# Halves of an exchange, and transposes by blocks, in a two-layer attention kernel on one Trainium2 core

## Chip, core and metric

The kernel runs on one core of one Trainium2 chip. All arithmetic is in 32-bit floats. The metric is device time in microseconds (us): 1245.21 in the median of three runs, 1244.89 to 1247.77.

## What is computed

Two layers act on x, 8 batches of 128 rows of 512. Layer 0 picks an adapter weight for each batch and adds a small mixture of low-rank experts. Layer 1 is attention with a paged cache of keys and values, and behind it a gated network; this is where the change lies:

```python
q = rmsnorm(x @ Wq.T, q_norm_w)          # 32 heads of 128
k = rmsnorm(x @ Wk.T, k_norm_w)          # 8 heads of 128
v = x @ Wv.T
q, k = rope(q, pos), rope(k, pos)
k_all = concat([k_cache[block_table], k])    # 512 cached + 128 new
v_all = concat([v_cache[block_table], v])
probs = softmax(where(valid, q @ k_all.T * SCALE, -1e30))
y = (probs @ v_all) @ Wo.T

scores = (y @ Wq_w.T) @ keys.T           # 64 experts, top 16
gate = softmax over the 16 best, 0 elsewhere
z_gated = (y @ A_w.T) * gate             # 8 columns for each expert
out = x + z_gated @ B_w.T * SCALING
```

## The kernel before

**Units.** Layer 0 takes the first 114 us or so. Then a loop runs over 64 units: a unit is one batch and one group of heads (four query heads with their key head). Two units make a step `st` (two groups, GH = 2); a step is one batch, and the 8 batches are gone through four times, once for each pair of groups. `iteration(u)` works on several units at once: scores and softmax of unit u (`scores`, `mask_exp`, `normalize`), norms and rotation of unit u + 3, the values of unit u - 2 (`values`, TensorE), and the output product of unit u - 3 (`evict_o` and `output`). In between, the projections of later units run on TensorE (`project`, seven products of halves instead of eight; L259, L262, L265). Iterations alternate: the even one has three of these products, the odd one four. An even one takes 15.9 us, an odd one 17.2 us.

**The exchange.** Probabilities have queries on partitions and TensorE wants them with keys on partitions. VectorE turns them in blocks of 32x32 (`blocks`, L833, 128x640 each, four heads) into the tile `pb`; the blocks of q and k for unit u + 2 go to the end of the same tile (`blocks_qk`, L784). `exchange_out` (L847) writes the tile to DRAM (`px`) with four transfers of 400 KB, two on SP's queue and two on ScalarE's, at the end of iteration u. `exchange_in` of the next iteration reads back `qkb` (L857, 320 KB) and `pT` (L860, 1280 KB) on SP. `heads_qk` (L867) copies qkb on ScalarE into the form that the scores take. `evict_o` (L891) is ScalarE's copy of the values' result out of PSUM, which the output product y (L902) needs; ScalarE comes to it behind its two px writes of the iteration before.

**SP's queue.** In every iteration SP issues, in this order: three transfers of the next step's keys (`gather`, L194, 32 KB each; 16 in a step, ten in an even and six in an odd iteration), qkb, pT, the rest of the gathers, a load of the running output in even ones (`load_y`, L143), its store (`add_output`, L926), and its two px writes. The values' rows come by GpSimd's indirect transfers (L204), and so do the weights of the next heads (wqkv, wo) in some iterations.

**The end.** For the last pair of groups a step's y is complete, and the gated network begins while the loop still runs: `f_turn` turns y by four TensorE transposes (L684) and a ScalarE copy (L686), `f_project` makes the expert scores and z (L692, L701), `f_gate` (L712 to L733, VectorE, with one exponential on ScalarE, L724) picks the experts and multiplies, `z_turn` turns z (L746, L748), and `f_second` makes the result (L1147). `LAST` says in which iteration each batch's part comes (u = 59 to 65); the last batch comes behind the loop. `TURNED`, `gate` and the functions `turn_*` are new.

Of the kernel before, what the change touches and what calls it, by code (L numbers as in the profile page):

```python
# [31 lines left out]
NQ = HKV // GH  # L32
HW = NH // 2 * D + D
QD = P // 32
PW = REP * (LC + 1) * 32
XW = PW + NH * 32
EPS = 1e-6
SCALE = D ** -0.5
E1, R1, RD = 64, 8, 16
# [18 lines left out]
def adaln_ffn_kernel(  # L58
# [124 lines left out]
    def gather(step, first=0, end=NPP):  # L183
        hf, b = divmod(step, B)
        if first == 0:
            kv_t[step] = (
                kvp.tile([P, NPP, GH, PSIZE], F32, tag="kt", name=f"kt_{step}"),
                kvp.tile([P, LC, GH * D], F32, tag="vt", name=f"vt_{step}", bufs=3),
            )
        kt, vt = kv_t[step]  # L190
        for j in range(first, end):
            at = b * NPP + j
            page = nc.sync.value_load(pg[0:1, at : at + 1])
            nc.sync.dma_start(  # L194
                out=kt[:, j, :, :].rearrange("p g t -> p (g t)"),
                in_=kc[hf, ds(page, 1)].rearrange("o p f -> p (o f)"),
            )
# [473 lines left out]
    def f_fold(psum):  # L671
# [5 lines left out]
            )  # L677
        nc.vector.tensor_copy(fw_t["s"], rk)

    def f_turn(b, sb, psum):  # L680
        yb = ya_t.pop((NQ - 1) * B + b)
        tp = psum("tp", [P, NC, S])
        for c in range(NC):
            nc.tensor.transpose(tp[:, c, :], yb[:, c * P : (c + 1) * P], ident)  # L684
        yT = sb("yT", [P, NC, S])
        nc.scalar.copy(yT, tp)  # L686
        return yT
# [52 lines left out]

    zT_t = {}

    def z_turn(b, tp, sb):
        zg = zg_t.pop(b)
        for c in range(NC):
            nc.tensor.transpose(tp[:, c * S : (c + 1) * S], zg[:, c * P : (c + 1) * P], ident)  # L746
        zT = sb("zT", [P, NC, S])
        nc.scalar.copy(zT.rearrange("p c s -> p (c s)"), tp)  # L748
        zT_t[b] = zT


    with ExitStack() as l1:
# [6 lines left out]
        )  # L759

        p_t, pb_t, pT_t, den_t, o_t, oT_t, y_t = {}, {}, {}, {}, {}, {}, {}
        mask_t, px_t, qkb_t, qk_out = {}, {}, {}, {}

        def make_mask(st):
            b = st % B
# [2 lines left out]
            mask_t[st] = m  # L768

        def new_pb(u):  # L770

            if u < 2:
                pb_t[u] = wk1.tile([P, QD, PW], F32, tag=f"pT{u}", name=f"pb_{u}")
                return
            pb_t[u] = wk1.tile([P, QD, XW], F32, tag="pb", name=f"pb_{u}")

        def blocks_qk(u, w):

            if w == 1:
                gap = xo[:, 0, 4:].rearrange("p x c s -> p (x c s)")[:, : NH * S]  # L780
                qk_out[w] = gap.rearrange("p (i f) -> p i f", i=QD)
            else:
                qk_out[w] = pb_t[w][:, :, PW:]
            nc.vector.transpose(  # L784
                qk_out[w].rearrange("p i (h a) -> p h i a", a=32),
                qk_t.pop(u).rearrange("p h t d -> p h (t d)").rearrange(
                    "p h (i a) -> p h i a", a=32
                ),
            )
# [40 lines left out]
        def blocks(u, h):  # L830

            w = (LC + 1) * 32
            nc.vector.transpose(  # L833
                pb_t[u][:, :, h * w : (h + 1) * w].rearrange("p i (j a) -> p j i a", a=32),
                p_t.pop((u, h)).rearrange("p (j i a) -> p j i a", i=QD, a=32),
            )

        def exchange_out(u):

            pb = pb_t.pop(u)  # L840
            m = dram_x.tile([QD, 32, QD, XW], F32, tag="px", name=f"px_{u}")
            w = XW if u + 2 in range(3, NU) else PW
            for i in range(QD):
                eng = nc.sync if i < QD // 2 else nc.scalar
                for n, end in ((PW, w), (0, PW)) if u == 1 else ((0, w),):
                    src = qk_out[u] if n else pb[:, :, :end]
                    (nc.sync if n else eng).dma_start(  # L847
                        out=m[:, :, i, n:end].rearrange("k b f -> b k f"),
                        in_=src[i * 32 : (i + 1) * 32],
                    )  # L850
            px_t[u] = m

        def exchange_in(u):
            m = px_t.pop(u).rearrange("k b i f -> (k b) i f")
            if u + 2 in range(3, NU):
                qkb = wk1.tile([P, QD, NH * 32], F32, tag="qkb", name=f"qkb_{u + 2}")
                nc.sync.dma_start(out=qkb, in_=m[:, :, PW:])  # L857
                qkb_t[u + 2] = qkb
            pT = wk1.tile([P, QD, PW], F32, tag=f"pT{u % 2}", name=f"pT_{u}")
            nc.sync.dma_start(out=pT, in_=m[:, :, :PW])  # L860
            pT_t[u] = pT

        def heads_qk(u):
# [46 lines left out]
        def add_output(u):  # L910
            st, g = units[u]
            del oT_t[u]
            if g % GH < GH - 1:
                return
            y = y_t.pop(st)
            last = st >= (NQ - 1) * B
            if g < GH:
                ya_t[st] = yp.tile([P, DM], F32, tag="ya", name=f"ya_{st}")
                nc.vector.tensor_copy(ya_t[st], y)
            else:  # L920

                t = y_home[st % B] if last and st % B < 4 else ya_t[st]
                nc.vector.tensor_tensor(t, y, ya_t[st], ALU.add)
                ya_t[st] = t
            if not last:
                nc.sync.dma_start(out=y_d[st % B], in_=ya_t.pop(st))  # L926

# [1 line left out]

        LAST = {NU - 5 + b: b for b in range(B - 1)}  # L930
        y_home, yT_t, room_t = {}, {}, {}

        def rooms():
            w = wp.tile([P, 7 * 2 * HW], F32, tag="wqkv", name="rooms", bufs=GH)
# [38 lines left out]
            (2, 3): (1, 1, 1),  # L973
        }

        def iteration(u):

            on = lambda v: 0 <= v < NU
# [17 lines left out]
            first, end = ((0, 10), (10, NPP))[u % GH]  # L996
            if pages:
                gather(st + 1, first, first + 3)
            if on(u - 1):
                exchange_in(u - 1)  # L1000
            if pages:
                gather(st + 1, first + 3, end)
            if pages:
                gather_v(st + 1, u % GH * LC // GH, (u % GH + 1) * LC // GH)
            if on(u + 3) and u % GH == 1:
                make_tables(units[u + 3][0])
            if u % GH == 0 and B <= st - 1 < NQ * B:
                load_y(st - 1)
            if on(u - 3):
                evict_o(u - 3)  # L1010
            if u >= NU and fb is not None:
                yT_t[fb] = f_turn(fb, *f)
            if u > NU:
                z = u - NU - 1
                z_turn(z, bank("q" if z else "kv", f"ztp_{z}"), lambda n, shape: y_home[
                    z
                ].rearrange("p (c s) -> p c s", c=NC))
            for h in range(REP):
                if on(u):
                    scores(u, h)  # L1020
                    mask_exp(u, h)
                    if h > 0:
                        normalize(u, h - 1)

                    if h == 1:
                        if u == 2:
                            rotate(4)
                        elif u == 3:
                            sums_q(1, 3, 2)
                        elif u == 4:  # L1030
                            sums_q(1, 4, 1)
                        elif r in (10, 11, 12, 13) and u < NU - 8:
                            sums_q(group + r // 12, *((3, 2), (4, 1))[r % 2])
                    if h == 2:
                        new_pb(u)
                        if u + 2 in range(3, NU):
                            blocks_qk(u + 2, u)
                    if h > 1:
                        blocks(u, h - 2)
                    if h == 1 and u == NU - 5:  # L1040
                        f_fold(f[1])
                    if h == 2 and fb is not None:
                        yT_t[fb] = f_turn(fb, *f)
                if on(u - 3):
                    output(u - 3, h)
                if h > 0 and slots:
                    project(k, j, slots[h - 1 : h])

                if (u, h) in WHOLE:
                    project_whole(1, *WHOLE[u, h])  # L1050
            if on(u - 3):
                add_output(u - 3)
            if on(u + 1) and (u + 1) % GH == 0:
# [21 lines left out]
            if on(u):  # L1075
                blocks(u, REP - 2)
                blocks(u, REP - 1)
                exchange_out(u)
            if 4 < u + 3 < NU:
                rotate(u + 3)  # L1080
                if four and slots:
# [6 lines left out]
                y_home.update({b: t[:, b * DM : (b + 1) * DM] for b in range(4)})  # L1088
            if u == NU - 6:
                rooms()  # L1090
            if fb is not None:
                f_gate(fb, *f_project(fb, yT_t.pop(fb), *f), *f)
            if on(u - 2):
                values(u - 2)

        make_mask(0)
# [5 lines left out]
    with ExitStack() as l2:  # L1102
# [31 lines left out]
        def f_turn_z(t):  # L1134
            b = t
            sb = lambda n, shape: p2.tile(shape, F32, tag=n, name=f"f{n}_{b}")
            z_turn(b, bank("q" if t % 2 else "kv", f"ztp_{t}"), sb)

        def f_second(t):
            b = t  # L1140
# [114 lines left out]
```

## Time and profile before

| | |
|---|---|
| median of three runs | 1245.21 us (1244.89 to 1247.77) |
| profiled execution | 1245.7 us |
| its span | 1243.9 us (1.8 us lie around it) |
| TensorE (PE) busy | 1225.7 us, 99% of the span, 3847 matmuls |
| VectorE (DVE) busy | 901.9 us, 73% |
| ScalarE (ACT) busy | 506.5 us, 41% |
| GpSimd (POOL) busy | 590.9 us, 48% |
| granted TensorE clock | 0.998 |
| moved by DMA | 298.99 MB in 205505 packets, 240 GB/s in the mean |

PE, DVE, ACT, POOL and SP are TensorE, VectorE, ScalarE, GpSimd and SyncE. A line such as `L847 ACTq DMA_DIRECT2D px<-pb` is the issue of a transfer on that engine's queue, from tile pb to tile px, by line 847. In the lists of groups the numbers behind x are counts, and behind the bar stand busy time, mean ns of one, and the idle time of the engine just before, with what ended most of it. In the list of waits the numbers are total us, times, longest us. In the list of issues the last number is the median from issue to landing.

### The profile page before, as it was taken

To read this page: it belongs to the slowest core of one execution; us is meant where nothing else is said; L and a number is where in the kernel's file an instruction comes from. 1 tells how busy PE (TensorE), PEld (TensorE's weight loads), DVE (VectorE), ACT (ScalarE), POOL (GpSimd) and SP (SyncE) were. 2 spreads that over 40 slices of the span, in tenths; PEclk is the share of its full clock that TensorE was granted. 3 is DMA by queue.
4 is the path that set the end of the run, shared out by engine and by line. 5 is a ranking of instruction groups with operands and counts; after the bars stand their busy time and mean duration, and the time that the engine had idled before them with its cause. 6 is when DMAs were issued, how large, how long until landed. Compare 5 with 4: busy or idle time off the path is not lost.

```text
span 1243.9 us, 15998 instructions
## 1 busy us (share of the span) xinstructions
PE 1225.7 (99%) x3847; PEld 651.1 (52%) x3847; DVE 901.9 (73%) x2045; ACT 506.5 (41%) x1457; POOL 590.9 (48%) x687
## 2 busy tenths in 40 slices
PE   8999899999999999999999999999999999999998
PEld 7765455554555555545555545554555555555444
DVE  3546788888877777788877777788777777777522
ACT  1334444444444444444444444444444444443211
POOL 2443565576544444565545545555555444543100
PEclk9999999999999999999999999999999999999999
DMA  8822777788877887788878878888888877787512
GB/s 302 304 78 94 229 234 245 245 274 281 269 243 245 272 258 239 259 295 278 269 248 267 264 221 258 294 272 267 257 268 262 255 243 233 246 261 269 179 51 85
DMA packets 205505, 298.99 MB, mean 240 GB/s; under 512 B 84643, under 2 KB 117156, under 8 KB 204516
## 3 DMA queue, kind: packets, MB, share of 16 engines
q1 hardware_dynamic: 173812, 205.58, 52.6%
q10 hardware_dynamic: 18720, 52.32, 12.0%
q0 software_dynamic: 12880, 40.08, 9.7%
q8 instruction: 31, 0.51, 0.2%
q14 instruction: 62, 0.51, 0.1%
HBM read 183.54 MB, written 114.36 MB: 239 GB/s over the span
## 4 chain that ended last, share of the span: by engine, by line
PE 89%; DMA 4%; DVE 2%; ACT 1%; issue 1%; POOL 1%; SPq 1%; ACTq 0%; DVEq 0%; POOLq 0%
PE o L880 19%; PE p L259 19%; PE y L902 17%; PE s L798 16%; PE s L801 4%; PE bp L517 2%; PE op L1147 2%; PE p L292 2%; PE cp L495 2%; PE fz L701 2%; DMA kt<-in_kc 1%; DMA bww<-in_base_w 1%; DMA px<-pb 1%; PE cp L512 1%; DMA pT<-px 1%
## 5 line engine op out<-in xcount | busy, mean ns | idle before, releaser
L828 POOL TENSOR_SCALAR p<-p,den 128x640 f32<-128x640 f32 x256 | 211.8, 827 | 424.4 <-DVE den L827 423.8
L822 ACT ACTIVATE p<-p,low 128x640 f32<-128x640 f32 x256 | 211.9, 828 | 436.3 <-DVE den L827 295.6
L811 DVE CUSTOM_DVE_ANT_0 p<-s,mask,rs 128x640 f32<-128x640 f32 x256 | 223.5, 879 | 108.8 <-PE s L801 106.1
L259 PE MATMUL p<-wqkv,xo 128*128 128x384 f32 x784 | 280.5, 487 | 0.0
L902 PE MATMUL y<-wo,oT 128*128 128x512 f32 x512 | 262.8, 598 | 7.6 <-ACT oT L891 7.4
L798 PE MATMUL s<-kt,qkT 128*128 128x512 f32 x504 | 258.9, 595 | 1.5 <-DVE low L811 0.8
L880 PE MATMUL o<-pT,vt 128*128 128x512 f32 x512 | 230.2, 593 | 0.0
L833 DVE STREAM_TRANSPOSE pb<-p 128x640 f32<-128x640 f32 x256 | 211.0, 824 | 16.9 <-POOL p L828 16.9
L259 PEld LDWEIGHTS p<-wqkv,xo 128*128 128x128 f32 x784 | 149.1, 190 | 139.8 <-issue 72.3
L801 PEld LDWEIGHTS s<-qkT 128*128 128x128 f32 x504 | 96.2, 191 | 121.0 <-issue 121.0
L880 PEld LDWEIGHTS o<-pT,vt 128*128 128x128 f32 x512 | 97.5, 190 | 110.1 <-issue 95.0
L204 POOL DMA_INDIRECT vt<-in_vc,vrow x128 | 136.3, 1065 | 37.4 <-issue 28.2
L798 PEld LDWEIGHTS s<-kt,qkT 128*128 128x128 f32 x504 | 95.4, 191 | 96.7 <-issue 54.0
L308 ACT ACTIVATE sq<-c 128x128 f32<-128x128 f32 x320 | 98.8, 309 | 8.1
L314 POOL TENSOR_TENSOR rs<-ss,mhalf 128x5 f32<-128x5 f32 x64 | 99.5, 1554 | 5.3
L801 PE MATMUL s<-qkT 128*128 128x128 f32 x504 | 97.2, 275 | 0.0
L891 ACT COPY oT<-o 128x512 f32<-128x512 f32 x64 | 37.4, 585 | 144.9 <-PE o L880 133.6
L902 PEld LDWEIGHTS y<-wo,oT 128*128 128x128 f32 x512 | 78.6, 192 | 14.2 <-ACT oT L891 9.7
L262 DVE TENSOR_TENSOR c<-c,p 128x384 f32<-128x384 f32 x84 | 45.3, 539 | 28.8 <-PE p L259 28.7
L880 PE MATMUL o<-pT,vn 128*128 128x512 f32 x128 | 65.4, 592 | 0.0
L308 ACT ACTIVATION_READ_ACCUMULATOR sq<-c 128x1 f32 x320 | 59.7, 187 | 0.0
L340 DVE SCALAR_TENSOR_TENSOR ca<-c,rs,tab 128x128 f32<-128x128 f32 x64 | 24.8, 387 | 45.1 <-POOL rs L314 45.1
(181 smaller groups left out, 1200.7 us busy)
## 6 DMA issues: line engine op xcount, KB each, us to landing
pT<-px SPq DMA_DIRECT2D x64, 1280.0 KB, 6.7
px<-pb ACTq DMA_DIRECT2D x120, 400.0 KB, 5.3
px<-pb SPq DMA_DIRECT2D x120, 400.0 KB, 5.5
qkb<-px SPq DMA_DIRECT2D x61, 320.0 KB, 3.5
kt<-in_kc SPq DMA_DIRECT2D x512, 32.0 KB, 4.4
wqkv<-in_wqkv POOLq DMA_DIRECT2D x32, 384.0 KB, 5.4
yd<-ya SPq DMA_DIRECT2D x24, 256.0 KB, 3.1
wo<-in_wo POOLq DMA_DIRECT2D x12, 512.0 KB, 4.7
```

Source lines behind the costliest of these rows:

```text
L204: nc.gpsimd.indirect_dma_start(out=kv_t[step][1][:, c, :], out_offset=None, in_=vc, in_offset=bass.IndirectOffsetOnAxis(ap=vrow[:, hf, at ...
L259: nc.tensor.matmul(out=ps, lhsT=xo[:, pr, x, c, :], rhs=w[:, c, :], start=(c == 0), stop=(c == 1))
L308: nc.scalar.activation(sq, cs[:, at : at + D], AF.Square, accum_out=ss[:, h : h + 1])
L314: nc.gpsimd.tensor_tensor(rs, ss, mhalf, ALU.pow)
L798: nc.tensor.matmul(out=s[:, :L], lhsT=qkT[:, h, :], rhs=kt[:, :, g % GH, :], start=True, stop=True)
L801: nc.tensor.matmul(out=s[:, L:NK], lhsT=qkT[:, h, :], rhs=qkT[:, REP, :], start=True, stop=True)
L811: nc.vector.tensor_tensor_reduce(out=p, in0=s_t.pop((u, h))[:, :NK], in1=mask_t[st], scale=rs_t[u][:, h : h + 1], scalar=BIG, op0=ALU.add, ...
L822: nc.scalar.activation(p, p, AF.Exp, bias=low, scale=-1.0, accum_out=den)
L828: nc.gpsimd.tensor_scalar(p_t[u, h], p_t[u, h], den, 1.0, ALU.mult, ALU.mult)
L833: nc.vector.transpose(pb_t[u][:, :, h * w : (h + 1) * w].rearrange("p i (j a) -> p j i a", a=32), p_t.pop((u, h)).rearrange("p (j i a) -> ...
L880: nc.tensor.matmul(out=o, lhsT=vt[:, c, j * D : (j + 1) * D] if c < LC else vn_t.pop(u), rhs=pT[:, c], start=(c == 0), stop=(c == LC),)
L902: nc.tensor.matmul(out=y_t[st], lhsT=oT_t[u][:, h, :], rhs=wo_t[g][:, h, :], start=(h == 0 and j == 0), stop=(h == REP - 1 and j == GH - 1),)
```

## The change

Four things change.

1. The tile pb becomes two: pb_a (the blocks of q and k, and heads 0 and 1) and pb_b (heads 2 and 3). The first half is written out in the iteration's fourth head, two transfers on SP and two on ScalarE; the second half at the end of the iteration on SP, and in the next iteration on ScalarE, behind `evict_o`. So eight writes take the place of four. In the next iteration SP reads qkb behind three gathers, and pT behind all of them.
2. Six of the eight y and six of the eight z are turned without TensorE: VectorE turns blocks, four SP transfers write them to DRAM in the next iteration, one reads them back, and a ScalarE copy puts them in order.
3. The gate of a batch comes an iteration later, behind head 1's mask exponential; from u = 64 on at the start, with the values of the last units ahead of the projections.
4. y is always added into its own tile; the first two units' blocks have no tiles of their own any more.

```diff
+TURNED = B - 2
+def turn_blocks(n, rows, room, pool):
+    nc.vector.transpose(
+        room.rearrange("p (k c a) -> p c k a", k=QD, c=NC),
+        rows.rearrange("p (c k a) -> p c k a", c=NC, k=QD),
+    )
+    blocks_t[n] = pool, room
+def turn_out(n):
+    pool, room = blocks_t.pop(n)
+    m = pool.tile([QD, 32, QD, NC * 32], F32, tag="yx", name=f"yx_{n}")
+    for i in range(QD):
+        nc.sync.dma_start(out=m[:, :, i].rearrange("k b f -> b k f"),
+            in_=room[i * 32 : (i + 1) * 32].rearrange("p (k f) -> p k f", k=QD))
+    return n, m, room
+def turn_in(n, m, room):
+    nc.sync.dma_start(
+        out=room.rearrange("p (i f) -> p i f", i=QD), in_=m.rearrange("k b i f -> (k b) i f"))
+    turned_t[n] = room
+def turn_chunks(n, out):
+    nc.scalar.copy(out.rearrange("p c (i a) -> p c i a", a=32),
+        turned_t.pop(n).rearrange("p (i c a) -> p c i a", i=QD, c=NC))
 def f_turn(b, sb, psum):
+    if ("y", b) in turned_t:
+        yT = sb("yT", [P, NC, S])
+        turn_chunks(("y", b), yT)
+        return yT
...
         def new_pb(u):
-            if u < 2:
-                pb_t[u] = wk1.tile([P, QD, PW], F32, tag=f"pT{u}", name=f"pb_{u}")
-                return
-            pb_t[u] = wk1.tile([P, QD, XW], F32, tag="pb", name=f"pb_{u}")
+            pb_t[u] = (
+                wk1.tile([P, QD, XA], F32, tag="pb_a", name=f"pba_{u}"),
+                wk1.tile([P, QD, XW - XA], F32, tag="pb_b", name=f"pbb_{u}"),
+            )
...
-        def exchange_out(u):
+        def exchange_out(u, half, engines=(nc.sync, nc.scalar)):
...
-            pT = wk1.tile([P, QD, PW], F32, tag=f"pT{u % 2}", name=f"pT_{u}")
+            pT = wk2.tile([P, QD, PW], F32, tag="pT", name=f"pT_{u}")
...
+        def gate(fb):
+            b = fb - 1
+            part, f = gate_t.pop(b)
+            f_gate(b, *part, *f)
+            if b < TURNED:
+                turn_blocks(("z", b), zg_t[b], spare[:, b * DM : (b + 1) * DM], dram_x)
 def iteration(u):
             if pages:
                 gather(st + 1, first, first + 3)
+            if on(u - 3):
+                evict_o(u - 3)
             if on(u - 1):
-                exchange_in(u - 1)
+                exchange_out(u - 1, 1, (nc.scalar,))
+                read_qk(u - 1)
             if pages:
                 gather(st + 1, first + 3, end)
+            if on(u - 1):
+                read_pT(u - 1)
+            out_now = [turn_out(n) for n in list(blocks_t)]
...
-            if on(u - 3):
-                evict_o(u - 3)
-            if u >= NU and fb is not None:
-                yT_t[fb] = f_turn(fb, *f)
...
+            if u >= NU:
+                gate(u - NU + 5)
             for h in range(REP):
...
                     if h > 1:
                         blocks(u, h - 2)
+                    if h == 3:
+                        exchange_out(u, 0)
...
-                    if h == 2 and fb is not None:
+                    if h == 1 and fb:
+                        gate(fb)
+                    if h == 0 and fb is not None:
                         yT_t[fb] = f_turn(fb, *f)
...
             if on(u):
                 blocks(u, REP - 2)
                 blocks(u, REP - 1)
-                exchange_out(u)
+                exchange_out(u, 1, (nc.sync,))
+            for t in out_now:
+                turn_in(*t)
+            b = (u - 3) // GH - (NQ - 1) * B
+            if on(u - 3) and (u - 3) % GH and 0 <= b < TURNED:
+                place = y_home[b] if b < 4 else spare[:, (b + 2) * DM : (b + 3) * DM]
+                turn_blocks(("y", b), ya_t.pop((NQ - 1) * B + b), place, dram_x)
...
+            if u >= NU and on(u - 2):
+                values(u - 2)
             if fb is not None:
-                f_gate(fb, *f_project(fb, yT_t.pop(fb), *f), *f)
-            if on(u - 2):
+                gate_t[fb] = f_project(fb, yT_t.pop(fb), *f), f
+            if u < NU and on(u - 2):
                 values(u - 2)
```

## The prediction

> **What bounds the kernel now.** First the busy times and the slices of the page.
>
> ```profile
> PE 1225.7 (99%) x3847; PEld 651.1 (52%) x3847; DVE 901.9 (73%) x2045; ACT 506.5 (41%) x1457; POOL 590.9 (48%) x687
> ...
> PEclk9999999999999999999999999999999999999999
> DMA  8822777788877887788878878888888877787512
> ```
>
> TensorE works 1225.7 of 1243.9 us at full clock: its idle time is 18.2 us in all. Only less TensorE work or some of these 18 us can be gained, and anything that makes TensorE wait costs in full. The transfers stand at 0.7 to 0.8 all through the attention. Next, TensorE's and SP's waits, and issue to landing:
>
> ```profile
> PE y L902 <- ACT oT L891: 7.4, 8, 2.6
> PE s L798 <- DVE low L811: 0.8, 1, 0.8
> ```
>
> ```profile
> pT<-px SPq DMA_DIRECT2D x64, 1280.0 KB, 6.7
> px<-pb ACTq DMA_DIRECT2D x120, 400.0 KB, 5.3
> px<-pb SPq DMA_DIRECT2D x120, 400.0 KB, 5.5
> kt<-in_kc SPq DMA_DIRECT2D x512, 32.0 KB, 4.4
> ```
>
> The largest wait is y (L902) for ScalarE's copy of values (L891). Where it comes from, ScalarE's timeline shows, at unit 3 and then later in the loop; the spread of the px issues (min/median/max, ns) stands behind it:
>
> ```profile
> 149.04 0.72 ACT L867 COPY qkT<-qkb 128x640 f32<-128x640 f32 x1 [2.43 <-DMA qkb<-px]
> ...
> 152.79 0.31 ACTq L847 DMA_DIRECT2D px<-pb  x1
> 153.14 0.59 ACT L891 COPY oT<-o 128x512 f32<-128x512 f32 x1 [1.04 <-DMA pT<-px]
> ```
>
> ```profile
> L847 ACTq DMA_DIRECT2D px<-pb x96: 310/390/2188, 202.3 to 987.6; - x96
> ```
>
> ScalarE issues its px writes ahead of the copy. A write usually takes 0.39 us to issue, but up to 2.19, and then the copy and y are late. The long ones have a cause in the built program: SP's and ScalarE's transfers take eight completion semaphores in turn, in one common order, and each waits until the eighth before it has landed. One late transfer so holds the queue of whoever comes eight places behind. SP's own timeline at unit 46 (x7: seven gathers in 5.39 us) shows what stands in its queue when the first halves are to go out, at about 851:
>
> ```profile
> 848.05 5.39 SPq L194 DMA_DIRECT2D kt<-in_kc  x7
> 854.39 0.33 SPq L143 DMA_DIRECT2D ya<-yd  x1
> 854.82 0.49 SPq L926 DMA_DIRECT2D yd<-ya  x1
> 855.40 0.38 SPq L847 DMA_DIRECT2D px<-pb  x1
> ```
>
> **What the change takes away.** (a) *Transposes.* Twelve groups of four go to VectorE. A group holds TensorE 0.435 us (it starts at 1229.16, the next matmul at 1229.60; 1094.51 to 1094.94 likewise): 12 x 0.435 = 5.2 us. One of them, f_turn(5) at 1174.94, stood in the time in which TensorE waits for the copy of values anyway, so it gives nothing; in exchange the wait of 0.29 at 1201.94 goes, behind the projection of output 6: 5.2 - 0.4 + 0.3 = 5.1. What replaces them is twelve stream transposes on VectorE (128x640 takes 0.824 us, so about 0.66 for 128x512), 48 + 12 transfers and twelve ScalarE copies of 0.585 us (L891's shape). They have at least one iteration of 16 us for a round trip of 3.1 + 3.2 us (yd, ya), so they lie beside TensorE. If that cover is gone, each late turn costs up to its round trip. SP's part stands behind read_pT and the second-half writes, from u = 52 on, five places more in the common order per output or product.
>
> (b) *The copy of values ahead of the second-half writes.* Of the eight waits, .68, .96 and .88 (at 555, 722 and 856) stand behind a slow px write: 2.5 us. The wait of 1.00 at 1108.6 stands behind the gate's exponential, which goes a turn later: 1.0. That at 289.0 (.73) stays: ScalarE there is only busy, and the first-half writes add as much ahead of it as the second-half writes take from behind. One of 0.29 stays too. Sum 3.5.
>
> (c) *Unit 3.* Its qkb landed at 149.0 and made ScalarE wait 2.43 us, then y 2.61. With q and k in the first half, written about 134, the copy L867 can run at about 147.8 and L891 at 151.3 instead of 153.1; then VectorE's rotation sets the scores. Between 1.5 and 4.4, taken 2.7. Units 1 and 2 have 0.06 us of room at VectorE, and may lose 0.5. Sum 2.2.
>
> (d) *Gates.* A gate is about 3.5 us of VectorE with ScalarE's exponential in it. It moves from ahead of the next iteration's first mask exponential to ahead of its third, in four iterations with scores (60 to 63). VectorE is done with head 0 there some 2.3 to 3.0 us before the score of head 2 needs its bank, and the gate stood before a mask exponential already: taken at nothing; if that cover is too short, 0.5 to 1.2 us four times. The last values and projections (u from 64) only change places: nothing. Adding into ya, and the first two units' blocks in pb instead of homes of their own: nothing, for x1d and xo are read long before (first mask exponential at 118.3).
>
> Together 10.8, say 11 us. The added packets (two pieces of 1920 and 1280 B for one of 3200) cost little: rows of 1280, 2560 and 3200 B in the trace fit 7.6 ns a packet, and 32768 packets more over 16 engines are 16 us of 1244, 1.3% of the DMA share.
>
> **What it adds.** The first-half writes of unit u on ScalarE go out in the middle of the iteration, and in the common order they now stand among SP's gathers. In the changed program, in every even iteration from the sixth on, the seventh of ten gathers waits until ScalarE's first write *of the same unit* has landed. That write comes after exponential 3, which ends 11.9 us after the iteration's first score (s0). Landing is 1.7 us later at best (the quickest kt) and 3.4 at worst (the quickest of all transfers from or to px), so L = s0 + 13.6 to 15.3; taken 14.8, near the px. Queued behind this gather on SP: three gathers, pT of the unit before, load_y, SP's own two first-half writes, yd, and the second-half writes. SP's early half is thus not early in even iterations. Step by step: pT goes out about L + 2 and lands 6.7 later, L + 8.7. The last second-half write waits for pT's place, and lands 5.4 later (px), L + 14.1. Gathers 14 and 15 of the next step's keys wait for that write; they go out within 0.4 to 0.9 and land 1.7 to 4.4 later: L + 16.2 to 18.4. At L = 14.8 that is s0 + 31.0 to 33.2; the keys are needed at the next even s0, 33.14 after the first (15.92 + 17.22, the two iterations). So the margin is +2.1 to -0.1. Where weights load it is less: two 384 KB pieces of wqkv or one of 512 KB of wo at 262 GB/s (the steady GB/s of the windows) are 2.0 to 3.0 us more. The middle, 32.1 + 2.5 - 33.1, is 1.5 us of TensorE wait in each of about 12 such pairs: 18 us (0 to 3.1 each: 0 to 37).
>
> A second wait is in every odd iteration: VectorE's blocks of q and k (L784) need pb_a free, whose last SP write lands at about L + 10.9 = 25.7 where VectorE is ready at 22.4. It stands 3.3 us, with the mask exponentials and the product sums queued behind it. The seventh product needs a bank that VectorE frees 0.3 us after it is asked for; between 0 and 0.8 us a pair, taken 0.2 because VectorE has some 3 us idle in such a pair (29.4 busy of 33.1): 27 x 0.2 = 5.4, at most 22.
>
> Sum against the profiled execution's 1245.7 us (span 1243.9 and 1.8 around it; 0.5 above the median of 1245.2): 1245.7 - 11 + 18 + 5.4 = 1258.1; less 0.5 it is **1258**.
>
> [...]
>
> **The rivals.** *The chain of places has room everywhere (faster).* For it: before, SP is already held by its own px (91.4 us of SP's waits for px at L857) and TensorE does not wait for one kt in the whole loop; the last gather landed 872.4 before a score at 872.9, and in another pair 9 us ahead. If L is 13.6, the last gather lands at 29.8 to 32.0, in the middle 30.9, and with 2.5 us for weights at 33.4: 0.3 us in 12 pairs. Then only the gains count, 1245.2 - 11 = 1234, perhaps -13 with (c) at its best: 1232 to 1241. It decides from L = 13.3 down, where 13.3 + 17.3 + 2.5 is 33.1.
>
> *The chain eats just the gains (no change):* stalls of 7 to 15 us in all, 1241.5 to 1248.9.
>
> *VectorE's wait in the odd iterations comes through (much slower).* If the score of head 2 or the seventh product waits the whole 0.8, with loads at 3 us, it is 22 + 37 - 11: 1293; 2.5 us a pair would be 1300. Against it: VectorE waits 106.1 us for scores (L811), so it has slack in most iterations.
>
> *It doesn't do what it says:* the SP half of the first-half writes goes out no earlier in even iterations, as worked out; that is in the forecast.
>
> **How the numbers follow.** 0.3% is 3.7 us, about what a measurement of this kernel can tell from no change. The forecast's case (chain at the edge, loads pay; own range 1249 to 1284) has 0.46; the chain with room 0.38; the wash 0.07; VectorE through 0.09. So faster 0.38, same 0.07, slower 0.55. The cases below 1241 hold 0.38, so the range starts inside them at 1233 and ends at 1284.
>
> **What would show it.** Right: kt or qkT as releasers of TensorE (L798) in pairs with weight loads; a gather of 3 us and more on SP before ScalarE's first px write has landed; L784 waiting about 3 us for px in odd iterations; TensorE busy about 5 us less; L891 without a px issue ahead of it, and its waits down from 7.4 to about 1.5 us. Wrong: TensorE's idle time stays under 15 us, then the chain had room; or y waits again for oT, then ScalarE's first-half writes made its norms late; or f_second (L1147) waits for a turned z, then the round trips don't fit.

## The result, and the profile after

The changed kernel takes 1318.5 us in the median of five runs (1317.0 to 1324.3), the kernel before 1247.2 in the five runs of the comparison (1244.9 to 1247.8): a ratio of 1.0589 with a 95% interval of 1.0562 to 1.0616. The change makes the kernel slower by 5.9%. The forecast was 1258, with a range from 1233 to 1284: the sign is right and the size is not. The sign owes something to luck: slower had a chance of 0.55, and 18 of the 23.4 us of new waits were for keys that TensorE did not wait for.

The profiled execution has a span of 1316.8 us against 1243.9. The page's busy times first:

```profile
PE 1246.0 (95%) x3799; PEld 650.6 (49%) x3799; DVE 905.1 (69%) x2057; ACT 505.1 (38%) x1457; POOL 576.4 (44%) x687
```

TensorE has 48 instructions fewer and is busy 20.3 us longer, and its idle time went from 18.2 to 70.8 us. Both together are the 72.9 us of the span. What it waited for is in its list of waits (us in total, times, longest):

```profile
PE p L261 <- DVE c L264: 44.1, 26, 2.7
PE s L838 <- ACT qkT L913: 5.7, 2, 3.9
PE y L948 <- ACT oT L937: 5.5, 6, 1.3
PE s L838 <- DVE low L851: 3.8, 6, 1.5
```

A new line stands on top: a product of the projections (L261) waits for VectorE's addition (L264), which frees its PSUM bank. Keys (kt), which the forecast's 18 us were for, do not appear at all. VectorE's own list says why it was late, and SP's list what stood behind that:

```profile
DVE pba L824 <- DMA px<-pba: 82.2, 30, 4.9
...
DVE pba L824 <- DMA kt<-in_kc: 17.0, 5, 4.9
DVE pba L824 <- DMA yd<-ya: 9.2, 4, 3.2
```

```profile
SPq L892 <- DMA pT<-px: 69.1, 18, 4.6
...
SPq L196 <- DMA pT<-px: 55.7, 29, 4.2
SPq L196 <- DMA px<-pba: 53.0, 31, 5.3
```

The blocks of q and k (L824) wait for the writes of pb_a, the first-half tile. Before, the same blocks (then L784) waited 7.5 us for px. SP waits 178 us, in these three lines, for transfers that bring the waiting transfer no data: a px write needs no pT, a gather neither pT nor px. These are waits for a place, that is, for one of the eight completion semaphores that the prediction describes. The records of both traces show them: before, the 1003 transfers of SP and ScalarE count on the same eight, 125 or 126 on each; after, 1315, with 164 or 165 on each; GpSimd's 187 count on eight others. All transfers of SP and ScalarE but the first eight (995 and 1307) came behind a wait of their queue for the semaphore that they take. In the lists of before, these are the blocks' line and the largest lines of SP for transfers without data for the waiter:

```profile
DVE pb L784 <- DMA px<-pb: 7.5, 7, 1.8
```

```profile
SPq L1123 <- DMA pT<-px: 4.9, 1, 4.9
SPq L143 <- DMA pT<-px: 4.4, 8, 0.9
```

The start of one iteration after another shows where the time is. From unit 4 to 58 the even iterations took 3.2 us more in sum, the 27 odd ones from 5 to 57 took **64.7 us** more (2.4 each; before 17.21 in all but six, after 18.1 to 23.3 from unit 7 on). Units 0 to 3 took 2.4 us less, 59 to 62 5.9 us more. One odd iteration, unit 37 (from 755.18, the even one before it from 739.26), in VectorE's, SP's and TensorE's timelines:

```profile
762.44 0.16 DVE L867 RECIPROCAL den<-den 128x1 f32<-128x1 f32 x1
766.37 0.84 DVE L824 STREAM_TRANSPOSE pba<-ca 128x640 f32<-128x640 f32 x1 [3.77 <-DMA px<-pba]
767.14 0.80 DVE L874 STREAM_TRANSPOSE pba<-p 128x640 f32<-128x640 f32 x1
767.86 0.52 DVE L264 TENSOR_TENSOR c<-u,p 128x384 f32<-128x384 f32 x1
```

```profile
752.79 3.70 SPq L196 DMA_DIRECT2D kt<-in_kc  x4
756.60 0.54 SPq L906 DMA_DIRECT2D pT<-px  x1
757.19 0.63 SPq L145 DMA_DIRECT2D ya<-yd  x1
757.92 1.13 SPq L892 DMA_DIRECT2D px<-pba  x2
```

```profile
765.52 1.45 PE L261 MATMUL p<-wqkv,xo 128*128 128x384 f32 x4
768.43 1.56 PE L261 MATMUL p<-wqkv,xo 128*128 128x384 f32 x4 [1.46 <-DVE c L264]
```

SP's half of the early writes leaves at 757.9, 18.7 us after the even score, behind gathers and pT. VectorE stands 3.77 us, until about 8 us after the second of these two writes was issued. Then it has 0.8 + 0.8 + 0.5 us of work in a row before the bank is free, and the seventh product starts 1.46 us late.

### The profile page after: what moved, and what is told of

Its sections match the earlier page's. It is cut to its first block, busy times and chain, and to the rows that moved or that the text cites. A ratio compares the mean times of both kernels' runs of the same rounds, so it can differ in the third digit from the quotient of the medians.

```text
span 1316.8 us, 16433 instructions
## 1 busy us (share of the span) xinstructions
PE 1246.0 (95%) x3799; PEld 650.6 (49%) x3799; DVE 905.1 (69%) x2057; ACT 505.1 (38%) x1457; POOL 576.4 (44%) x687
## 4 chain that ended last, share of the span: by engine, by line
PE 36%; DMA 31%; DVE 11%; issue 9%; SPq 5%; ACT 5%; POOL 3%; ACTq 1%; DVEq 0%; POOLq 0%
DMA px<-pba 20%; PE o L926 8%; PE p L261 6%; PE s L838 5%; PE y L948 5%; DMA pT<-px 4%; DVE pba L874 3%; ACT sq L310 3%; PE bp L519 2%; PE op L1217 2%; PE cp L497 2%; DMA kt<-in_kc 2%; PE p L294 2%; DMA yd<-ya 2%; POOL rs L316 2%
## 5 line engine op out<-in xcount | busy, mean ns | idle before, releaser
L261 PE MATMUL p<-wqkv,xo 128*128 128x384 f32 x784 | 295.3, 501 | 44.1 <-DVE c L264 44.1
L851 DVE CUSTOM_DVE_ANT_0 p<-s,mask,rs 128x640 f32<-128x640 f32 x256 | 220.3, 876 | 43.7 <-PE s L841 41.7
L261 PEld LDWEIGHTS p<-wqkv,xo 128*128 128x128 f32 x784 | 148.9, 193 | 194.6 <-issue 76.3
L926 PE MATMUL o<-pT,vt 128*128 128x512 f32 x512 | 237.4, 607 | 0.0
L926 PEld LDWEIGHTS o<-pT,vt 128*128 128x128 f32 x512 | 101.4, 198 | 116.7 <-issue 103.7
L824 DVE STREAM_TRANSPOSE pba<-ca 128x640 f32<-128x640 f32 x61 | 51.2, 840 | 111.0 <-DMA px<-pba 82.2
L874 DVE STREAM_TRANSPOSE pbb<-p 128x640 f32<-128x640 f32 x128 | 106.8, 835 | 22.3 <-POOL p L868 22.2
L874 DVE STREAM_TRANSPOSE pba<-p 128x640 f32<-128x640 f32 x128 | 104.3, 814 | 5.5 <-DMA px<-pba 5.2
L314 POOL TENSOR_SCALAR ss<-ss,eps 128x5 f32<-128x5 f32 x64 | 33.0, 516 | 123.8 <-ACT sq L310 123.8
L316 POOL TENSOR_TENSOR rs<-ss,mhalf 128x5 f32<-128x5 f32 x64 | 76.6, 1197 | 5.3
```

What stands on the lines that cost most here:

```text
L261: nc.tensor.matmul(out=ps, lhsT=xo[:, pr, x, c, :], rhs=w[:, c, :], start=(c == 0), stop=(c == 1))
L316: nc.gpsimd.tensor_tensor(rs, ss, mhalf, ALU.pow)
L851: nc.vector.tensor_tensor_reduce(out=p, in0=s_t.pop((u, h))[:, :NK], in1=mask_t[st], scale=rs_t[u][:, h : h + 1], scalar=BIG, op0=ALU.add, ...
L874: nc.vector.transpose(pb[:, :, at : at + w].rearrange("p i (j a) -> p j i a", a=32), p_t.pop((u, h)).rearrange("p (j i a) -> p j i a", i=Q ...
L926: nc.tensor.matmul(out=o, lhsT=vt[:, c, j * D : (j + 1) * D] if c < LC else vn_t.pop(u), rhs=pT[:, c], start=(c == 0), stop=(c == LC),)
```

## The experiments

Times are medians; the ratio is to the runs of before on the same chip.

**Four arrangements of the exchange.** The first theory, A, was the prediction's: the order of transfers. Its rival B was volume: 45000 more packets.

ScalarE's early half moved to the next iteration:

```diff
-exchange_out(u, 0)                        # at head 3
+exchange_out(u, 0, (nc.sync,))
 # next iteration, behind evict_o
+exchange_out(u - 1, 0, (nc.scalar,))
 exchange_out(u - 1, 1, (nc.scalar,))
```

> As the changed kernel, but ScalarE's two first-half writes go out in the next iteration, behind the copy of values, with its second-half writes; only SP's two stay early. Theory A (order of transfers): in the changed kernel ScalarE's early write stands among SP's gathers in the common order of transfers, so in even iterations SP's own first half goes out only at s0 + 19 and behind pT, pb_a comes free at about s0 + 27 and VectorE's q and k blocks wait 3.8 us in odd iterations; here no gather waits for a write of its own unit, the waits of L824 for px fall from 82 us to under 25 us, odd iterations fall from 18.3-22.4 to 17.2-18.5 us, and the time is 1235 to 1260 us. Theory B (volume: eight writes and 45000 more packets make all transfers later, whatever their order): stays at 1300 to 1320 us, L824's wait above 60 us.

Measured: 1319.3 us, 1.0591 (1.0563 to 1.0619). L824 waited 68.2 us for px. Theory A in this form failed.

Both halves at the end of the iteration:

```diff
-    if h == 3:
-        exchange_out(u, 0)
 ...
+exchange_out(u, 0)
 exchange_out(u, 1, (nc.sync,))
```

> As the changed kernel with its two tiles and eight writes, but all first-half writes go out at the end of the iteration, right ahead of SP's second-half writes; ScalarE's second half still behind the copy of values. Theory A: pb_a comes free about where pb did before, L824 waits little, odd iterations 17.2 to 18 us, time 1235 to 1252 us. Theory B: the same number of writes and packets, so 1300 us or more.

Measured: 1315.6 us, 1.0547 (1.0508 to 1.0586). Eight writes at the old moment cost as much as eight at the new one.

pT behind the early writes:

```diff
-if on(u - 1):
-    read_pT(u - 1)
 for h in range(REP):
     ...
+if on(u - 1):
+    read_pT(u - 1)
```

> As the changed kernel, with one move: pT of the unit before is read behind the early first-half writes instead of ahead of them. Theory A: ScalarE's early write still holds SP's gathers, but SP's first half no longer stands behind a transfer of 1280 KB (6.7 us to land), so pb_a comes free 4 to 6 us earlier and L824's wait (3.8 us in the changed kernel) is all but gone: 1234 to 1255 us. Theory B: 1300 us or more. If only the holding of the gathers counted and not the queue behind them, L824's wait would stay above 2 us and the time above 1285.

Measured: 1371.8 us, 1.1035 (1.0983 to 1.1086). VectorE's wait at L824 did go: 2.2 us are left of it. But others came: y for oT 26.2 us, scores for qkT 19.5. Taking one transfer out of the way put it into another's. None of the three new orders brought anything back; whether some other order would, they don't show.

The exchange of before, with the rest of the change:

```diff
-pb_a, pb_b; exchange_out(u, 0); exchange_out(u, 1, ...)
+pb; exchange_out(u)                       # four writes, end of iteration
```

> The changed kernel with the exchange of before (one tile, four writes of 400 KB at the end of the iteration, qkb and pT read behind three gathers, copy of values behind ScalarE's writes); the six turned outputs, the six turned products and the later gates stay. By the prediction's terms this is worth 5.1 us of TensorE's transposes and 1.0 us of the wait at 1108: 1238 to 1243 us, odd iterations 17.2 us as before. If the rival is right that the turned copies or the gates cost at the end, it is 1248 us or more; with Theory A or B alone the loss of 71 us lies wholly in the exchange.

Measured: 1247.5 us, 1.0011 (0.9997 to 1.0025). The 71 us lie in the exchange. The 6 us that the rest promised did not show either: units 0 to 3 took 2.4 us more (in this version the first units' blocks have no homes of their own), and 55 and 57 4.6 us more. These are figures of the profiled execution, which at 1252.4 us is the slowest of ten, 4.9 above the median.

**Packets or number of transfers?** Theory C: SP's and ScalarE's transfers share eight completion places, and each waits for the eighth before it, so more transfers mean waiting for younger ones. A pair of units has 30 such transfers before (16 gathers, 8 px, 2 qkb, 2 pT, ya and yd) and 38 after.

The kernel before with SP's px writes in three pieces:

```diff
-to.dma_start(out=m[:, :, i, n:end]..., in_=src[i * 32 : (i + 1) * 32])
+for a, e in ((0, 16), (16, 24), (24, 32)):     # on SP only
+    to.dma_start(out=m[:, a:e, i, n:end]..., in_=src[i * 32 + a : i * 32 + e])
```

> The kernel before, with each of SP's two px writes cut by rows into three (16, 8 and 8 partitions): eight writes a unit instead of four, as in the changed kernel, but with the same packets of 3200 B, the same tile, the same place at the end of the iteration. Theory A (order) is in doubt since three other orders of the halves cost as much (1316, 1319 and 1372 us). Theory B (volume: packets): nothing changes in packets, so 1243 to 1250 us. Theory C (places: SP and ScalarE share eight completion places, and four more transfers a unit push every later one to wait for transfers that were issued less time ago): 1270 to 1330 us, with odd iterations longer.

Measured: 1402.7 us, 1.1255 (1.1226 to 1.1285). More transfers with the same packets do the damage, beyond the range given, and TensorE waits at the same place as in the changed kernel, for the bank of a product:

```profile
PE p L259 <- DVE c L262: 77.5, 26, 4.7
```

The pieces are smaller, too, 200 and 100 KB for 400 KB; what that adds, this run does not separate.

The changed kernel and the kernel before with merged gathers:

```diff
-for j in range(first, end):
-    page = nc.sync.value_load(pg[0:1, at : at + 1])
-    nc.sync.dma_start(out=kt[:, j, :, :]..., in_=kc[hf, ds(page, 1)]...)
+nc.sync.dma_start(out=kt[:, first:end]..., in_=kc[hf, first:end]...)
```

> The changed kernel with each run of gathers as one transfer (3, 7 or 3 pages, taken from consecutive pages, so the block table is left out of the computation): 4 gathers in a step instead of 16, bytes and packets as in the changed kernel. Theory C: twelve places fewer a step outweigh the eight that the halves added; the waits of L824 for px fall under 20 us and the time to 1232 to 1250 us. Theory B: 1300 us or more.

> The same edit on the kernel before, as the control: the same bytes and packets with twelve transfers fewer a step. Both theories: 1236 to 1247 us, since TensorE waits little there; at most the slow px issues ahead of the copy of values (2.5 us) and part of unit 3 go.

Measured: 1237.7 us, 0.9935 (0.9909 to 0.9961), and 1242.9 us, 0.9966 (0.9941 to 0.9990). With the changed kernel's bytes and px packets, but fewer transfers, the whole loss is gone; all but a few odd iterations are 17.21 us again. Theory B falls. The change on its own terms, with places to spare, is worth 5.3 us here.

**Which of the places?** Theory D was SP's time to issue. Theory E keeps the places, but lays the loss on one wait among them, that of a gather for ScalarE's early write. The same merge with the register loads kept:

```diff
 nc.sync.dma_start(out=kt[:, first:end]..., in_=kc[hf, first:end]...)
+for j in range(first, end):
+    nc.sync.value_load(pg[0:1, b * NPP + j : b * NPP + j + 1])
```

> The changed kernel with all gathers merged, but SP still loads the page numbers into its registers, one load for each page behind the transfer (their values are unused; the block table is left out of the computation). If SP's time to issue (Theory D) made the loss, a good half of a gather's 0.85 us stays, 16 times a step, and the time stays above 1270 us. Theories C and E: as with the gathers merged without the loads, 1236 to 1245 us.

Measured: 1238.9 us, 0.9932 (0.9909 to 0.9954). The loads cost about a microsecond, so SP's time for them is not short. The issues themselves, 0.33 us each in the median, went with the merge, so this run says nothing of them.

ScalarE's second-half writes on GpSimd's queue:

```diff
-eng = nc.sync if i < QD // 2 else nc.scalar
+eng = nc.sync if i < QD // 2 else nc.gpsimd if half else nc.scalar
```

> The changed kernel with ScalarE's two second-half writes of each unit issued on GpSimd's queue, whose transfers have completion places of their own: SP's instructions, bytes, packets and the order on SP stay as they are, and the shared places per pair of units fall from 38 to 34 (before: 30). Theory C (places): part of the loss comes back, 1255 to 1300 us, with SP's waits for transfers that bring it no data (L892 and L196 for pT, L196 for px, 178 us in the changed kernel) well down. Theory D (SP's time to issue, some 0.4 to 0.8 us an instruction, is what is short): SP issues as much as before, so 1310 us or more. Theory B (packets): 1310 us or more.

Measured: 1325.1 us, 1.0619 (1.0584 to 1.0655): a miss for Theory C as a mere count, and in the range of theories D and B, which the merged gathers speak against. SP's timeline of this run, in an even iteration:

```profile
753.29 8.20 SPq L196 DMA_DIRECT2D kt<-in_kc  x7
761.68 0.53 SPq L906 DMA_DIRECT2D pT<-px  x1
...
762.97 1.18 SPq L892 DMA_DIRECT2D px<-pba  x2
```

In the built program gathers still wait for ScalarE's early write of the same unit, here issued at 756.5 (80.7 us of SP's waits are gathers for px from pba, 53.0 in the changed kernel), so the seven take 8.2 us and SP's first half again leaves late. It matters which transfer stands eight places ahead.

Merged gathers in even iterations alone, and in odd ones alone:

```diff
+if first < 10:        # c_even_one;  first >= 10: c_odd_one
+    nc.sync.dma_start(out=kt[:, first:end]..., in_=kc[hf, first:end]...)
+    return
 for j in range(first, end):
```

> The changed kernel with the gathers of even iterations alone as one transfer for each run of pages (2 instead of 10; pages taken in a row, so the block table is left out there); odd iterations keep their six. This takes away the one place wait that the prediction named: the seventh gather of an even iteration waiting for ScalarE's early write of the same unit, with pT and SP's first half queued behind. Theory E (places, and within them this wait): L824's wait for px falls under 30 us, most odd iterations are 17.2 us again, 1236 to 1260 us. If the waits are spread over all transfers (Theory C in its plain form), 1260 to 1290 us. GpSimd's run, where four places fewer a pair brought nothing, speaks for E.

> The counterpart: the gathers of odd iterations as 2 transfers instead of 6, even iterations keep their ten (block table left out in the odd ones). Theory E: the wait of the even iterations stays, so 1290 us or more and L824 waits over 50 us. Plain Theory C: four places fewer a pair, 1280 to 1310 us.

Measured: 1243.4 us, 0.9975 (0.9956 to 0.9994), and 1265.9 us, 1.0161 (1.0133 to 1.0190). Eight places fewer in the even iterations bring back all of the loss, as Theory E said, and the blocks of q and k (L830 in these two kernels) no longer wait. Their line among VectorE's groups (idle before them last) shows 0.0 us, against 111.0 in the changed kernel:

```profile
L830 DVE STREAM_TRANSPOSE pba<-ca 128x640 f32<-128x640 f32 x61 | 50.3, 825 | 0.0
```

But four fewer in the odd ones bring back 53 of 71 us, where E allowed at most 28 and plain C at most 38: the blocks' wait for px was still there, with 35.6 of 82.2 us. In that build, however, the order had shifted: up to unit 52, what waits for ScalarE's early write in even iterations is pT, ya or a px write, and no gather. So this run took away the wait that the prediction named too, and some 20 us stayed: that wait is not all, and how large a part it is neither run isolates.

**Parts of the change worth keeping?** First the turned products alone, with the later gates, y on TensorE and the exchange of before:

```diff
-exchange_out(u, 0); exchange_out(u, 1, ...)
+exchange_out(u)                            # as before, first units' homes too
-turn_blocks(("y", b), ya_t.pop(...), place, dram_x)
+t = y_home[st % B] if last and st % B < 4 else ya_t[st]
```

> The kernel before with the gates a turn later and the six gated products turned by blocks; exchange, homes of the first units and the turning of y as before. The run with the old exchange and all of the turns gave 1247.5 us, where the terms promised 6 us less than before: it lost 3.0 us at unit 2 (no homes of their own for the first blocks) and 4.6 us at units 55 and 57, where turned outputs pass through SP beside weight loads. Without these two, the terms are six groups of 0.435 us, 2.6 us, and 1.0 us of the wait at 1108: 1240 to 1244 us. If the turned products also wait somewhere, 1246 us or more.

Measured: 1261.7 us, 1.0136 (1.0110 to 1.0161): a miss. In the profiled execution, which is 8.6 us above the median, units 29 and 45 lost 7.6 us together against before, and 60 to 62 13.1 us, where y goes through TensorE again while the gates come later; the products of the expert scores (L733) waited 9.2 us for ScalarE's copy of y.

Then all turns and later gates, with halves for units 0 to 2 alone:

```diff
+if h == 3 and u < 3:
+    exchange_out(u, 0)
 ...
+exchange_out(u, 1 if u < 3 else None)     # None: four whole writes
```

> The turned outputs, turned products and later gates of the change, with halves for units 0 to 2 alone; from unit 3 on four whole writes at the end of the iteration, copy of values and reads as before. By the steps so far: units 2 and 3 take 17.1 and 19.8 us (39.3 before, 41.7 with the old exchange throughout), the rest as the run with the old exchange, 1247.5 - 4.8 = 1243 us; the wait at unit 57 stays.

```diff
-if on(u - 3) and (u - 3) % GH and 0 <= b < TURNED:          # h_start
+if on(u - 3) and (u - 3) % GH and 0 <= b < TURNED and b not in (1, 2):   # h_start_skip
```

> The same with outputs 1 and 2 turned by TensorE as before, so that SP has no turned output at units 55 and 57, where the old exchange lost 0.8 and 3.9 us: 1243 - 4.6 + 0.9 = 1239 us, ahead of both kernels, if the places there are the cause; 1243 if the weight loads of the gated network are.

Measured: **1240.5 us, 0.9959 (0.9939 to 0.9980)**, ahead of both kernels, and 1244.7 us, 0.9997 (0.9980 to 1.0015). The wait at unit 57 was gone without any step against it (17.21 us). Whether it came from the order that the other build happened to have, or from its slow profiled execution, is open. The second lost 2.9 and 4.3 us against before at units 60 and 61, with y on TensorE again.

Last, ScalarE's whole writes behind its copy of values, on top of the better one:

```diff
-exchange_out(u)                               # SP and ScalarE, end of iteration
+exchange_out(u, None, (nc.sync,))
 # next iteration, behind evict_o
+exchange_out(u - 1, None, (nc.scalar,))
```

> The version with halves for units 0 to 2 alone (1240.5 us) and, of the change, also ScalarE's two whole writes behind its copy of values from unit 4 on. By the prediction's term (b) the waits of y for oT at 555, 722 and 856 go: 2.5 us less, 1238 us. But the writes leave about 1 us later and ScalarE's two issues then stand ahead of nothing that counts; if the later landing of qkb or the places eat it, 1241 us or more.

Measured: 1281.6 us, 1.0292 (1.0259 to 1.0325), 41 us worse than without this part. VectorE's list of waits:

```profile
DVE pb L821 <- DMA px<-pb: 60.2, 32, 4.3
```

From unit 3 on there are no halves here and no more px writes than before. ScalarE's writes leave later (in one iteration at 755.4 and 755.7, behind the copy at 755.0), pb comes free later, and VectorE waits in odd iterations as in the changed kernel. The order of places changes with them, too: SP's own px writes wait 50.2 us for other px writes, where the kernel before has 1.7 us. The run does not tell the one from the other:

```profile
SPq L888 <- DMA px<-pb: 50.2, 14, 5.5
```

## Why the prediction was wrong, point by point

**The gains, 11 us: about half.** The cleanest measure is the pair of kernels with merged gathers, in which places are to spare: the change gains 5.3 us there. In the changed kernel itself only the 2.4 us of units 0 to 3 are to be seen, and units 59 to 62 took 5.9 us more.

**(a) Transposes, 5.1 us: seen in part.** In the better version's profiled execution (2.7 us below its median) the span is 8.2 us shorter than before (1235.7), of which 2.2 are units 0 to 3, 1.6 the odd iterations, and about 4.7 lie from unit 59 on, where (a) and the later gates were to bring 6.1. With the old exchange the part from unit 59 on is 1.6 us shorter, and no run has the turns alone.

**(b) The copy of values ahead of the writes, 3.5 us gained: the price is missing.** y's wait went from 7.4 to 5.5 us, not to 1.5, and the term had no price for writes that leave later. On the better version, which has no halves from unit 3 on, the same move cost 41 us, by the later writes and by the order of places together; what it cost in the changed kernel no run shows. This is the first step that failed: of a step that is moved back, whoever waits for its landing has to be asked too.

**(c) Unit 3, 2.2 us: right.** Units 0 to 3 took 2.4 us less.

**The chain of places: nearly right up to VectorE.** SP's first half left 18.7 us after the even score, VectorE was let go at about 27.1 where 25.7 was worked out, and stood 3.77 us where 3.3 was. The second write let VectorE go some 8 us after its issue, where the sum had 5.4 for its landing.

**What that costs TensorE: the step that made the miss.** The forecast took 0.2 us a pair, 5.4 us, since VectorE had 3 us idle in the pair; the odd iterations measured 2.4 a pair, 64.7 us, of which 44.1 are TensorE's 26 waits for the bank. The idle time was no cover: it lies elsewhere in the pair, and VectorE began nothing during the wait (in unit 37 from 762.60 to 766.37); the addition came after it, at 767.86. The wait should have been carried on to the next thing that TensorE needs: by the prediction's own working the bank was to be late by 0.3 us with the wait already in, and the trace shows 1.46 in a plain pair, with VectorE let go 1.4 us later than worked out. In this pair, then, what the write landed later came through to TensorE almost whole. This was the rival "VectorE's wait comes through", at 1293 to 1300 and with a chance of 0.09; its 2.5 us a pair is close, but it kept all 11 us of gains.

**The keys, 18 us: did not happen.** No wait of TensorE for kt is in the list. In units 25, 27, 29, 41, 43 and 45, beside weight loads, the odd iteration grew by 2.6 to 4.6 us, against 0.7 to 2.5 in the other odd ones from 13 to 53; TensorE waited for the bank there, as in the others, and its clock fell, in each of the six to 0.50 for 3.4 us. That the loads made these waits longer is likely, but no run leaves them out.

**The clock: had no term.** 28 of the 73 us are longer matmul times (1246.0 us busy against 1217.8 in the better version, with as many instructions). The granted clock, 0.986 of full speed over 1316.8 us against 1.000 there, makes some 18 of them by an estimate (0.014 of 1316.8); what made the other 10 is open.

**Slips in the working.** In the built program the gather that waits for ScalarE's first write of its unit is the eighth of ten, not the seventh, up to unit 52. In the chain of the keys 14.1 + 0.9 + 4.4 is 19.4 where 18.4 stands; with it the term would have been 24 us instead of 18. The trace before has packets of 640, 2560 and 3200 B, none of 1280; they took 32, 102 and 126 to 135 ns in the median, by which a packet costs some 8 ns besides its bytes. None of this bears on the miss.

Open is how the loss divides among single places. Each build orders its transfers anew, so no run here moves one place and leaves the rest.

## What to carry to other kernels

Here the transfers of two queues shared eight completion places in program order, and each took one, whether it moved 32 KB or 1280 KB. With 38 instead of 30 transfers a pair and the same packets, the kernel before took 12.6% longer; with twelve fewer, the changed kernel took 1237.7 us instead of 1318.5. So count transfers as well as bytes before splitting one or moving one early; a list of waits of the issuing queue that names a transfer with no data for the waiter (178 us in the changed kernel) shows who pays. VectorE's 3 us of idle time in a pair did not cover its wait of 3.77 us: idle time covers a new wait only if it lies between that wait and the next thing that the bounding engine needs, so follow the wait to that thing before taking a share of it. A write that is moved behind something else should be charged to whoever waits for its buffer (VectorE, with 60.2 us, in the last run).

## What the runs showed of the hardware that was not expected

TensorE's clock fell near the end of some waits of 1.5 to 3.9 us. In unit 25 of the changed kernel the seventh product waited 2.08 us; stretches of TensorE's windows around it (granted clock third from the end):

```profile
538.38:549.00 10.62, 10.62 (x34) 5.65 (x33) 4.98 (x14) 3.70 (x9) 7.17 (x8) 1.00 0.98 317
549.00:552.00 3.00, 1.17 (x4) 0.38 (x2) 1.81 (x3) 0.00 (x0) 0.00 (x0) 1.00 0.72 244
552.00:559.63 7.63, 7.38 (x14) 3.46 (x15) 5.56 (x12) 3.85 (x14) 5.29 (x6) 0.78 0.84 246
```

```profile
552.25 1.88 PE L261 MATMUL p<-wqkv,xo 128*128 128x384 f32 x4 [2.08 <-DVE c L264]
553.92 5.02 PE L926 MATMUL o<-pT,vt 128*128 128x512 f32 x8
```

The clock was 0.78 for the next 7.6 us: the eight value matmuls took 5.02 us where they took 3.60 in unit 37, and the product 1.88 for 1.45. Inside that stretch the granted clock was 0.50 from 553.4 to 556.8; eleven such stretches of 3.4 us at half the clock lie in this execution, one in that of the kernel before, ahead of its last microsecond. Of the 4.04 us that this iteration grew, 2.08 are the wait and 1.85 the longer matmuls, some 1.7 of these by the clock (0.22 of 7.63). After the 1.46 us wait of unit 37 the value matmuls kept their pace. The length of a wait alone does not decide: after 2.22 us in unit 21, at 482.0, the granted clock stayed at 1.00, and after 1.50 us at 1258.0 it was 0.79 over 8 us.

In the first 10.6 us of that iteration, beside weight loads, the DMA engines were busy 0.98 of the time, at 317 GB/s. What full engines add to the waits for places no run separates; unit 55, beside which no weights load, grew most of all, by 5.2 us.
